# A graph network on one core: list products spread over a chunk, and nine subtractions moved to GpSimd

## The chip, the cores and the metric

The kernel runs on one core of one Trainium2 chip. What is compared is the device time of one execution, in microseconds. Four compute engines matter here: TensorE (PE in the profile), VectorE (DVE), ScalarE (ACT) and GpSimd (POOL); SyncE (SP) only issues transfers. Each engine works through its own queue in order and waits where an instruction needs another engine's or a transfer's result.

## The reference

The graph has 2708 nodes with 512 features each and a symmetric 0/1 matrix `adj` in which about 0.6% of the entries are ones. Four layers follow each other, and each ends with a residual sum and a layer norm. Layers 0, 1 and 3 are plain graph convolutions. The change touches layer 2, which is attention applied twice:

```python
def _gat_layer(x, W, adj):
    proj = x @ W
    Wh, Ws = jnp.split(proj, 2, axis=-1)
    scores = Wh @ Ws.T
    a = jax.nn.softmax(scores, axis=-1) * adj
    out = a @ Wh
    out = out + x
    return jax.nn.leaky_relu(out, NEG_SLOPE)
```

The softmax runs over all 2708 columns before the mask is applied, so all scores are needed; only the product `a @ Wh` can use that the masked matrix is nearly empty.

## The kernel before

**Chunks and stages.** The nodes are cut into 22 row blocks of 128 (the last one has 20 rows), and a score matrix is made in six column chunks of 512, 512, 512, 512, 384 and 276 (`CH`). `Attention.layer` runs once for each of the two attention layers and walks the chunks k = 0 to 5; this text calls the work of one chunk a stage. In stage k three things are interleaved in one written order:

- The **scores** of chunk k. Chunks 0 to 4 use a scheme with seven products in place of eight for a pair of row blocks (`pair_steps`), ten pairs in a stage; each pair yields twice "mid" and twice "end", and other work is put in at these points. Some of the summed weights are not kept in SBUF but streamed back in each stage by `load_sums` (the transfers `s<-sums`).
- The **softening** of chunk k-1 (`soften`), one row block at a time: VectorE subtracts the chunk's column maxima (`shift`) from the scores, ScalarE takes the exponential one or two steps later, VectorE adds the result to the running sum and multiplies it with the mask, and SyncE writes the block to DRAM (`pairs<-s`). There are 26 steps (`SOFT`), the first at about the fourth end of the stage, the last near its end.
- The **list products** of chunk k-2 (`weigh`). For each block of 128 columns, lists of neighbours were worked out earlier. `fetch` gathers, for one list, 128 rows of `pairs` by an indirect transfer from GpSimd's queue (`g<-pairs,givers`), and `weigh` multiplies the gathered weights with the gathered rows into an accumulator (`acc<-g`). A block has four lists that stand alone and two groups of four, so six products and twelve gathers; a chunk of 512 has four blocks, 24 products and 48 gathers. `end` scales the finished block and adds the residual on VectorE.

So the products of a chunk can't begin before the whole chunk was softened and written, which is at the end of the stage before.

**The written order.** The program keeps a clock of its own (`advance`, `self.clock`), which adds an estimate for each TensorE product, 0.85 us for a single list and 1.1 us for a group. `fetch` puts down when a gather should have landed: 1.15 us after the gather before it, plus 6, and for the first gather of a chunk 16 us more. `weigh` puts a product into TensorE's queue only if that estimate has passed, and it is called up to three times at each "end". At most ten gathers stand ahead of their products (`AHEAD = WIDES - 1`, with eleven buffers). A gather's buffer is that of the gather eleven before it, so on the chip it also waits for that one's product. The clock sets only the order of the queues; what runs when is decided by the waits.

**The rest of the layer.** In stage 5 and after it (called the tail here) there is the softening of chunks 4 and 5 and the lists of chunks 3 to 5. Between them the first layer's tail puts the projections of the second layer (`second`), and the second layer's tail the first products of the last graph layer (`early`). The softening of chunk k writes into the DRAM buffer that chunk k-2's gathers read, so it waits for these in the written order (`while self.chunks[ch.k - 2].to_fetch`, and `chunks[-3]` in the tail).

Of the kernel before, what the change touches and what calls it, by code (L numbers as in the profile page):

```python
# [22 lines left out]
NB = 22  # L23
# [458 lines left out]
def pairs_of(k):  # L482


    return {4: (1, P), 5: (1, P)}.get(k, (2, 2 * P))


STREAMED = 4
SOFT = NB + 2 * 2
ALONE = 18  # L490
SEVEN = [k for k in range(len(CH)) if CH[k][1] >= 384]
# [884 lines left out]
class Chunk:  # L1376


    def __init__(self, ly, k):
        self.ly, self.k, self.cw = ly, k, CH[k][1]  # L1380
        self.name = f"{ly.number}_{k}"
        self.blocks = blocks_of(k)
        self.s, self.masks, self.ends = {}, {}, []
        self.half = self.cw // 2
        self.seven = k in SEVEN
        self.part, self.complete, self.ready, self.top = {}, [], [], None
        self.softened = 0
        self.apart = 2 if self.seven else 1
        self.fetched, self.rden = [], None
        self.x, self.first = {}, {}  # L1390
        self.rows = set()
        self.mv = None

        self.to_weigh = []
        for q, (i, _, _) in enumerate(self.blocks):
            ts = lists_of(i)
            self.to_weigh += [(q, t, t is ts[0], t is ts[-1]) for t in ts]
        self.to_fetch = [(q, t) for q, ts, _, _ in self.to_weigh for t in ts]
        self.first_fetch = self.to_fetch[0]
# [9 lines left out]
class Attention:  # L1409
# [7 lines left out]
    def __init__(self, fast):  # L1417
        self.f, self.k, self.nc = fast, fast.k, fast.nc
        self.page, self.bank = fast.page, fast.bank
        tc = self.k.tc  # L1420
        self.scratch = self.k.ctx.enter_context(
            tc.tile_pool(name="pairs", bufs=1, space=DRAM)
        )

        self.pairs = [
            [
                self.scratch.tile([NP, 2 * PAIR + D], FP, tag=f"p{a}{b}", name=f"pairs{a}{b}")
                for b in range(2)  # L1430
            ]
            for a in range(2)
        ]
        self.mixed = self.scratch.tile([DC, P, D], FP, tag="mixed", name="mixed")
        self.quarter = [
            [
                self.scratch.tile(
                    [2, P, pairs_of(k)[0] * P], FP, tag=f"q{a}_{k}", name=f"quarter{a}_{k}"
                )
                for k in range(len(CH))  # L1440
            ]
            for a in range(2)
        ]
        self.sums = [
            [
                self.scratch.tile([3, P, 2, 2 * P], FP, tag=f"u{a}_{k}", name=f"sums{a}_{k}")
                for k in range(STREAMED)
            ]
            for a in range(2)
        ]  # L1450
        self.layers = [AttentionLayer(a, self.pairs[a]) for a in range(2)]
        self.clock, self.fetch_free, self.pending = 0.0, 0.0, []
        self.left = None


    def blank(self):
# [140 lines left out]
    def sum_weights(self, ly, k):  # L1597
# [6 lines left out]
        names = ("s1", "s2", "s4")  # L1604
        if k < STREAMED:
            ly.streamed[k] = [self.page(f"{n}_{a}_{k}", FP, (P, 2, wide)) for n in names]
# [273 lines left out]
    def soften(self, ch):  # L1880


        nc, v, cw = self.nc, ch.softened, ch.cw
        ch.softened += 1
        if v < NB:
            n = rows_of(v)
            s = ch.s[v][:n, :cw]
            nc.vector.tensor_sub(s, s, ch.shift[:n, :cw])
        j = v - ch.apart
        if 0 <= j < NB:  # L1890
            s = ch.s[j][: rows_of(j), :cw]
            nc.scalar.activation(s, s, AF.Exp)
        j -= ch.apart
        if j < 0:
            return
        if j == NB - 1:
            ch.softened = SOFT
        if j == 0 and ch.k >= 2:
            while self.chunks[ch.k - 2].to_fetch:
                self.weigh(True)  # L1900
        if j % DC == 0 and j + 2 * DC < NB:
            self.load_mask(ch, j // DC + 2)
        n = rows_of(j)
        s = ch.s[j][:n, :cw]
        if j == 0:
            ch.sum = self.page(f"sum{ch.name}")
            nc.vector.tensor_copy(ch.sum[:, :cw], s)
        else:
            nc.vector.tensor_add(ch.sum[:n, :cw], ch.sum[:n, :cw], s)
        nc.vector.tensor_mul(s, s, ch.masks.pop(j)[:n, :cw])  # L1910
        to = ch.ly.pairs[ch.k % 2][j * P : j * P + n, :]
        if cw == BANK:
            nc.sync.dma_start(
                to[:, : 2 * PAIR].rearrange("j (r x) -> j r x", x=PAIR)[:, :, D:],
                ch.s[j][:n, :].rearrange("j (r x) -> j r x", x=2 * P),
            )
            return
        for r in range(2):
            w = min(2 * P, cw - r * 2 * P)
            nc.sync.dma_start(  # L1920
                to[:, r * PAIR + D : r * PAIR + D + w],
                ch.s[j][:n, r * 2 * P : r * 2 * P + w],
            )
# [17 lines left out]
    def fetch(self, ch):  # L1941


        q, t = ch.to_fetch.pop(0)
        g = self.f.wide(f"g{ch.name}_{q}_{t}")
        i, _, w = ch.blocks[q]

        for b in (q, q + 1):
            self.load_rows(ch, b)

        h = t // ONLY if t < QUARTERS * ONLY else (QUARTERS - 1, 0)[q % 2]
        first, width = (D + P + h * QW, D + P - h * QW) if q % 2 else (0, D + (h + 1) * QW)
        self.nc.gpsimd.indirect_dma_start(
            out=g[:, :width],
            out_offset=None,
            in_=ch.ly.pairs[ch.k % 2][:, :],
            in_offset=bass.IndirectOffsetOnAxis(ap=self.k.givers[:, i, t : t + 1], axis=0),
            element_offset=(q // 2) * PAIR + first,
        )

        begin = max(self.fetch_free, self.clock + (16 if (q, t) == ch.first_fetch else 0))
        self.fetch_free = begin + 1.15
        ch.fetched.append((g, self.fetch_free + 6))

# [8 lines left out]

    def fetch_ahead(self):
        count = sum(len(c.fetched) for c in self.chunks)
        for c in self.chunks:
            while c.to_fetch:
                if c.softened < SOFT or count >= self.AHEAD:
                    return
                self.fetch(c)  # L1980
                count += 1
# [11 lines left out]
    def weigh(self, wait=False):  # L1993

        nc = self.nc
        self.fetch_ahead()
        ch = next((c for c in self.chunks if c.to_weigh), None)
        if ch is None:
            return False
        q, ts, first, last = ch.to_weigh[0]  # L2000
        if len(ch.fetched) < len(ts):
            return False
        if ch.fetched[len(ts) - 1][1] > self.clock and not wait:
            return False
        ch.to_weigh.pop(0)
        if ch.rden is None:
            self.divisor(ch)
        w = ch.blocks[q][2]
        gs = [ch.fetched.pop(0)[0] for _ in ts]
        if first:  # L2010
            ch.acc = self.bank(1, f"acc{ch.name}_{q}")
            if ch.ly.number == 1:
                ch.first[q] = self.page(f"x1{ch.name}_{q}")
                self.nc.sync.dma_start(ch.first[q][:w], self.k.saved[1][ch.blocks[q][0]][:w])
        for h, g in enumerate(gs):
            lo, m = (0, w) if len(gs) == 1 else (h * QW, QW)
            e, z = (0, P - lo) if q % 2 else (D + lo, 0)
            nc.tensor.matmul(
                ch.acc[lo : lo + m],
                g[:, e : e + m],  # L2020
                g[:, z : z + D],
                start=first,
                stop=last,
            )
        self.advance(cost(D) if len(gs) == 1 else 1.1)
        if last:
            a = (ch, q, ch.acc, ch.x.pop(q), ch.first.pop(q, None))
            self.later(1.5, lambda: self.end(*a))
        self.fetch_ahead()
        return True  # L2030
# [86 lines left out]
    def layer(self, ly, chunks, fill):  # L2117
        f = self.f
        self.chunks, self.made = chunks, {}
        for k, ch in enumerate(chunks):  # L2120
            old = chunks[k - 1] if k else None
            following = chunks[k + 1] if k + 1 < len(chunks) else None

            n = -1
            for what in self.walk(ch):
                if what == "mid":
                    if old and n >= 3 and old.softened < SOFT:
                        self.soften(old)
                    continue
                n += 1  # L2130
                if old and n < 2:
# [19 lines left out]
                        self.restore(ly, i)  # L2151
                self.greatest(ch)

                for _ in range(3):
                    if not self.weigh():
                        break
                if old and n == 2:
                    self.shift_rows(old)
                if old and n == 3:
                    self.shift_columns(old)  # L2160
            assert not old or old.softened == SOFT
        last = chunks[-1]
        self.load_mask(last, 0)
        self.load_mask(last, 1)
# [122 lines left out]
```

## Time and profile before

| | |
|---|---|
| time, median of 3 runs | 2297.17 us (2293.18 to 2298.72) |
| the profiled execution's own time | 2341.13 us |
| its span | 2339.0 us |
| TensorE, share of the span | 96% |
| VectorE, ScalarE, GpSimd | 66%, 31%, 31% |
| granted TensorE clock, mean | 0.985 |
| first attention layer, stages 0 to 5 begin at | 761.5, 829.4, 900.8, 1005.0, 1107.2, 1184.2 us |
| second attention layer, stages 0 to 5 begin at | 1467.6, 1532.2, 1605.8, 1710.8, 1813.3, 1888.9 us |

The stages' beginnings are the first matmuls of each chunk's block 18, which is computed alone, or of block 0 in stage 5. A line of the table by stages, as the prediction shows it, gives a stretch of the execution, its length, then for each engine the time that it was busy and the number of its instructions that began in it, the granted TensorE clock, the mean busy share of the sixteen DMA engines, and the GB/s that they moved. In a line of the timeline the last bracket is the time that the engine stood idle ahead of the instruction, and what ended the wait; "issue" means nothing that the profile shows. As nearly all operations are recorded through one helper, all have its line number (L71), and they are told apart by the tiles that they write and read.

### The profile page before, as it was taken

How to read it: one execution, taken by the hardware profiler on the slowest of the kernel's cores; microseconds unless marked ns; L12 is line 12 of the kernel's file. 1: busy time of each engine (PE TensorE's matmuls, PEld its weight loads, DVE VectorE, ACT ScalarE, POOL GpSimd, SP SyncE). 2: the span in 40 equal slices, each digit the busy share in tenths (PEclk: the TensorE clock that was granted, in tenths of full speed). 3: DMA queues.
4: the chain of work that ended last, by engine and by line, in shares of the span. 5: the costliest groups of instructions: out<-in, count | busy, mean ns of one | idle time of the engine just before them, and what ended most of it. 6: DMA issues, size and time to landing. Idle time of an engine off the chain costs nothing.

```text
span 2339.0 us, 29486 instructions
## 1 busy us (share of the span) xinstructions
PE 2237.2 (96%) x9724; PEld 1515.8 (65%) x9724; DVE 1547.5 (66%) x3180; ACT 725.9 (31%) x1654; POOL 717.8 (31%) x827
## 2 busy tenths in 40 slices
PE   9999999999999998999999999998998997899997
PEld 6776876777545786566764345787565763466685
DVE  6777787777655679778784512579888896354523
ACT  7444452222111243233332101243233332251221
POOL 2433521111000002635566450002634564643000
PEclk9999999999999999999999999999999998999999
DMA  9966752223576426968899998426978899884311
GB/s 346 283 186 189 205 148 76 79 77 115 194 262 253 157 77 205 335 218 318 293 362 360 341 399 333 169 78 210 330 243 286 307 306 343 265 249 148 110 47 42
DMA packets 285139, 523.27 MB, mean 224 GB/s; under 512 B 42926, under 2 KB 134758, under 8 KB 284976
## 3 DMA queue, kind: packets, MB, share of 16 engines
q1 hardware_dynamic: 216320, 306.34, 37.9%
q0 software_dynamic: 68656, 214.96, 27.6%
q8 instruction: 78, 1.28, 0.2%
q14 instruction: 85, 0.70, 0.1%
HBM read 335.34 MB, written 185.83 MB: 223 GB/s over the span
## 4 chain that ended last, share of the span: by engine, by line
PE 71%; DVE 13%; issue 6%; DMA 6%; ACT 2%; POOL 1%; SPq 1%; another core or an unknown queue 0%; DVEq 0%; ACTq 0%; POOLq 0%
PE acc L71 27%; PE spx L71 10%; PE mm L71 8%; PE spy L71 8%; PE z L71 6%; PE wst L71 6%; DVE s L71 5%; PE sp L71 3%; DVE sum L71 2%; DMA at<-in_adj_t 1%; DVE top L71 1%; DMA g<-pairs,givers 1%; DMA x<-in_x 1%; DMA x<-x 1%; DVE r L71 1%
## 5 line engine op out<-in xcount | busy, mean ns | idle before, releaser
L71 POOL DMA_INDIRECT g<-pairs,givers x510 | 535.8, 1051 | 912.5 <-issue 359.3
L71 PE MATMUL acc<-m,xh 128*128 128x512 f32 (+4 forms) x1584 | 566.1, 379 | 8.4 <-issue 7.0
L71 PE MATMUL acc<-m,xl 128*128 128x512 f32 (+4 forms) x1584 | 549.5, 365 | 11.0 <-DVE xl L71 9.4
L71 PEld LDWEIGHTS acc<-m,xh 128*128 128x128 f32 (+1 forms) x1584 | 288.1, 188 | 71.9 <-issue 28.6
L71 PEld LDWEIGHTS acc<-m,xl 128*128 128x128 f32 (+1 forms) x1584 | 288.3, 188 | 54.7 <-DVE xl L71 10.4
L71 PE MATMUL acc<-g 128*32 128x512 f32 (+1 forms) x1020 | 285.0, 610 | 12.2 <-DMA g<-pairs,givers 7.5
L71 PE MATMUL mm<-w,ht 128*128 128x512 f32 (+1 forms) x528 | 223.3, 593 | 0.0
L71 ACT CAST m<-at 128x512 fp32r<-128x512 uint8 (+5 forms) x396 | 199.1, 567 | 40.2 <-DMA at<-mask 20.1
L71 PE MATMUL spx<-xs,wst_sb 128*128 128x256 f32 (+1 forms) x800 | 201.3, 375 | 9.2 <-DVE s L71 9.1
L71 PEld LDWEIGHTS spx<-xs,wst_sb 128*128 128x128 f32 x800 | 149.3, 193 | 47.2 <-issue 14.8
L71 DVE TENSOR_TENSOR s<-s,shift 128x512 f32<-128x512 f32 (+3 forms) x264 | 162.4, 619 | 24.7 <-ACT shift L71 14.4
L71 ACT ACTIVATE s<-s 128x512 f32<-128x512 f32 (+3 forms) x264 | 152.0, 582 | 84.8 <-DVE s L71 74.7
L71 DVE TENSOR_TENSOR s<-s,a 128x512 f32<-128x512 f32 (+3 forms) x264 | 166.0, 629 | 18.5 <-issue 9.5
L71 PEld LDWEIGHTS acc<-g 128*32 128x32 f32 (+1 forms) x1020 | 79.7, 136 | 148.5 <-issue 107.4
L71 PEld LDWEIGHTS mm<-w,ht 128*128 128x128 f32 (+1 forms) x528 | 95.8, 186 | 116.6 <-issue 112.3
L71 ACT COPY s<-spx 128x256 f32<-128x256 f32 (+1 forms) x300 | 106.0, 361 | 196.0 <-PE spx L71 143.5
L71 DVE TENSOR_TENSOR sum<-sum,s 128x512 f32<-128x512 f32 (+4 forms) x252 | 156.3, 620 | 4.1 <-ACT s L71 4.1
L71 DVE TENSOR_TENSOR top<-top,s 128x512 f32<-128x512 f32 (+4 forms) x240 | 149.6, 623 | 13.7 <-ACT s L71 9.6
L71 PE MATMUL z<-w,xt 128*128 128x512 f32 (+1 forms) x352 | 151.4, 596 | 0.0
L71 PE MATMUL wst<-xt,mixed 128*128 128x512 f32 (+2 forms) x384 | 150.9, 545 | 0.0
L71 PE MATMUL spy<-xs,wst_sb 128*128 128x256 f32 (+1 forms) x480 | 121.9, 377 | 9.4 <-DVE s L71 9.2
L71 PE MATMUL sp<-xs,wst_sb 128*128 128x276 f32 (+5 forms) x512 | 129.1, 460 | 0.0
(190 smaller groups left out, 2686.3 us busy)
## 6 DMA issues: line engine op xcount, KB each, us to landing
pairs<-z_sb SPq DMA_DIRECT2D x84, 768.0 KB
pairs<-s SPq DMA_DIRECT2D x168, 256.0 KB
s<-sums SPq DMA_DIRECT2D x96, 256.0 KB
at<-in_adj_t SPq DMA_DIRECT2D x84, 256.0 KB
xres<-x POOLq DMA_DIRECT2D x44, 256.0 KB
x<-o POOLq DMA_DIRECT2D x43, 256.0 KB
pairs<-s SPq DMA_DIRECT2D x84, 128.0 KB
a<-mask SPq DMA_DIRECT2D x40, 256.0 KB
```

Of the source, the lines that this page charges most:

```text
L71: ins = call(*args, **kw)
```

## The change

- Subtractions: of the 22 blocks of chunks 0 to 3 (512 columns, `STREAMED = 4`), the blocks 4, 6, ..., 20 (`OTHERS`, nine of them) are subtracted on GpSimd. The instruction is put into GpSimd's queue four softening steps before VectorE would have done it (`OTHERS_AHEAD`).
- Spacing: in stages 2, 3 and 4 (`SPACING`) a list product may not be written before `next_list`, which advances by 1.5, 1.5 or 1.2 us of the written clock for each list of a product. In these stages products are also written at "mid", one each, and two in place of three at "end".
- Gathers: in these stages at most six stand ahead of their products in the written order, in place of ten (`EVEN_AHEAD`). The number of buffers stays eleven.
- The first gather of a chunk, in all stages, is taken to land 5 us late in place of 16 (`FIRST_LANDS`).

```diff
+OTHERS, OTHERS_AHEAD = range(4, NB - 1, 2), 4
+FIRST_LANDS = 5
+SPACING, EVEN_AHEAD = {2: 1.5, 3: 1.5, 4: 1.2}, 6
...
+        self.others = set(OTHERS) if k < STREAMED else ()
...
-            nc.vector.tensor_sub(s, s, ch.shift[:n, :cw])
+            if v not in ch.others:
+                nc.vector.tensor_sub(s, s, ch.shift[:n, :cw])
+            if v + OTHERS_AHEAD in ch.others:
+                s = ch.s[v + OTHERS_AHEAD][:, :cw]
+                nc.gpsimd.tensor_sub(s, s, ch.shift[:, :cw])
...
-        begin = max(self.fetch_free, self.clock + (16 if (q, t) == ch.first_fetch else 0))
+        begin = max(self.fetch_free, self.clock + (FIRST_LANDS if (q, t) == ch.first_fetch else 0))
...
+        most = EVEN_AHEAD if self.spacing else self.AHEAD
...
-                if c.softened < SOFT or count >= self.AHEAD:
+                if c.softened < SOFT or count >= most:
...
+        if self.spacing and not wait:
+            if self.clock < self.next_list:
+                return False
+            self.next_list = max(self.next_list, self.clock - 2) + self.spacing * len(ts)
...
+            self.spacing = SPACING.get(k, 0.0)
             for what in self.walk(ch):
                 if what == "mid":
                     if old and n >= 3 and old.softened < SOFT:
                         self.soften(old)
+                    self.weigh()
                     continue
...
-                for _ in range(3):
+                for _ in range(2 if self.spacing else 3):
                     if not self.weigh():
                         break
```

More of the change, by code (lines that the diff above doesn't have):

```diff
@@ L1453, in __init__ @@
         self.left = None
+        self.spacing, self.next_list = 0.0, 0.0
     def blank(self):
@@ L2161, in layer @@
             assert not old or old.softened == SOFT
+        self.spacing = 0.0
         last = chunks[-1]
```

## The prediction

> **What bounds the kernel now.** The page first: TensorE is busy for 96% of the span, so the question is where its time isn't products. The stage table comes next (stages 1 to 5 of the first attention layer, then two pieces of its tail).
>
> ```profile
> PE 2237.2 (96%) x9724; PEld 1515.8 (65%) x9724; DVE 1547.5 (66%) x3180; ACT 725.9 (31%) x1654; POOL 717.8 (31%) x827
> ...
> 829.40:900.80 71.40, 66.71 (x305) 55.04 (x304) 61.87 (x104) 31.77 (x75) 0.00 (x0) 1.00 0.35 107
> 900.80:1005.00 104.20, 96.20 (x409) 65.47 (x408) 83.62 (x142) 30.59 (x74) 51.23 (x48) 0.95 0.79 279
> 1005.00:1107.20 102.20, 97.11 (x425) 66.40 (x424) 78.79 (x134) 32.64 (x78) 49.54 (x48) 0.98 0.82 288
> 1107.20:1184.20 77.00, 72.73 (x394) 58.34 (x394) 63.79 (x115) 29.62 (x78) 40.92 (x38) 0.96 0.85 304
> 1184.20:1245.00 60.80, 59.70 (x272) 40.18 (x271) 51.34 (x108) 20.40 (x50) 37.38 (x35) 1.00 0.98 357
> 1245.00:1320.00 75.00, 69.17 (x213) 29.76 (x211) 39.04 (x94) 15.88 (x36) 39.35 (x39) 0.95 0.96 342
> 1320.00:1467.60 147.60, 147.60 (x446) 65.39 (x445) 31.51 (x61) 13.59 (x28) 46.44 (x49) 1.00 0.95 359
> ```
>
> A stage has a floor. Stage 0 of the second layer, with nothing but scores, takes 64.6 us and is 64.56 busy. Three single lists take 2.68 us in the chain (0.87 each; a group and two singles 2.91, so the group about 1.2): 24 products are 16 x 0.87 + 8 x 1.2 = 23.5. With 3 us of transposes, stages 2 and 3 need 91 us and take 104.2 and 102.2; in the second layer 105.0 and 102.5. Stage 1 needs 65 and takes 71.4 and 73.6. Some 60 us are lost in all, and stage 4 adds to it.
>
> How they are lost: cutting stage 1 and the start of stage 2 into tens shows VectorE full, and a later ten shows it idle beside full DMA engines.
>
> ```profile
> 860.00:870.00 10.00, 10.00 (x48) 8.81 (x47) 9.82 (x17) 5.58 (x14) 0.00 (x0) 1.00 0.65 196
> 901.00:911.00 10.00, 6.17 (x21) 3.60 (x20) 9.76 (x18) 1.71 (x4) 0.00 (x0) 1.00 0.39 125
> ...
> 971.00:981.00 10.00, 6.58 (x26) 3.23 (x24) 2.58 (x4) 0.90 (x2) 6.72 (x7) 0.97 0.92 307
> 981.00:991.00 10.00, 9.25 (x25) 6.29 (x26) 9.22 (x15) 3.41 (x9) 5.18 (x5) 0.69 0.99 364
> ```
>
> TensorE's timeline names the waits, GpSimd's its rhythm:
>
> ```profile
> 910.82 1.13 PE L71 MATMUL spx<-xs,wst_sb 128*128 128x256 f32 x4 [3.83 <-DVE s L71]
> 981.75 2.08 PE L71 MATMUL spy<-xs,s 128*128 128x256 f32 x4 [3.77 <-issue]
> 1024.75 1.65 PE L71 MATMUL spy<-xs,s 128*128 128x256 f32 x3 [3.38 <-issue]
> 1809.87 1.65 PE L71 MATMUL spx<-t,wst_sb 128*128 128x256 f32 x3 [4.66 <-ACT v L71]
> ...
> 1142.52 0.95 POOL L71 DMA_INDIRECT g<-pairs,givers  x1 [17.87 <-PE acc L71]
> 1975.59 0.95 POOL L71 DMA_INDIRECT g<-pairs,givers  x1 [18.99 <-PE acc L71]
> ```
>
> So there are two kinds. VectorE is late (first and fourth line; ScalarE's queue holds exponentials that wait for VectorE's subtractions). And the streamed sums (tile s in `spy<-xs,s`, the third product) come late in stretches where gathers come in a burst: the ten from 971 moves 307 GB/s, and at 1024 eleven gathers had just been issued back to back. That it is these transfers is my reading; the view says only "issue". GpSimd's 17.87 us is the other face: eleven gathers at once, then none until the first product.
>
> **What the Trainium skill says.** "SBUF — State Buffer", section Who interferes with whom: a VectorE instruction with two SBUF inputs contends with a GpSimd instruction that reads SBUF; the second to start blocks for the whole of the first. No trace row shows this pair: where GpSimd multiplied before (`xt<-xt,dg`), VectorE ran `ht<-acc,xt`, which has one input in PSUM, and both kept their times. "GPSIMD Engine Reference", section 3.1, gives about 2.6 cycles an element for such an operation; the trace agrees (first line below: 512 columns in 1289 ns, and 276 in 776, hence 2.2 ns a column). "TensorE: Matmul & The Clock Gate", section What's actually happening: after an idle window of about 3.4 us the clock halves. The trace agrees: 3.77 us of waiting, then 0.69 in the next ten. "Trainium Kernel Development and Optimization", section Key Constraints: transfers of all queues share the sixteen DMA engines; the table's 0.92 to 0.99 with sums late fits.
>
> ```profile
> L71 POOL TENSOR_TENSOR xt<-xt,dg 128x512 f32<-128x512 f32 x16 | 20.2, 1289 | 27.0 <-DVE cnt_sb L71 27.0
> L71 DVE TENSOR_TENSOR s<-s,shift 128x512 f32<-128x512 f32 x168 | 114.0, 682 | 23.5 <-ACT shift L71 14.4 <-issue 9.1
> ```
>
> **The change, part by part.**
>
> *Subtractions.* VectorE loses 9 x 0.60 = 5.4 us a stage (0.60 is what one takes from start to start in the timeline; 0.68 is its latency), in eight stages. GpSimd gains 9 x (1.25 + 0.1). Without contention that is 5.4 us off a full VectorE. With the exclusive port, 82% of VectorE's busy time in stage 1 is in two-SBUF-input operations (50.7 of 61.5: subtractions, sums, mask products, maxima, `s<-s,v`), so a GpSimd subtraction costs VectorE 0.82 x 1.25 = 1.03 us and saves 0.60: a loss of 3.8 a stage. On the path this counts in stage 1 of both layers, where VectorE is full from 850 to 911. Bounds for both: -11 and +8. I take -2: the page states the block outright, but a GpSimd instruction also starts inside VectorE's short gaps and one-input operations. GpSimd's queue: a subtraction stands behind gathers that wait only for products five or more back, so it isn't held; four steps are some 8 us of lead. Gathers behind it come 1.35 us later, hidden by those already landed.
>
> *Spacing.* Reckoned by the written clock, the products of stages 2 and 3 lay from 24 to 78 of 86 us and now begin at 11. With six ahead, a second group of four finds two of its gathers outstanding; the other two land 2 x 1.15 + 6 = 8.3 us later by the estimate, so group follows group by 10 us, not 6, and a block takes 24. Three blocks fit in stage 2, not four: 6 products are carried out of it, 10 out of stage 3, 18 out of stage 4 (7 before) and 19 out of stage 5 (13 before). Gathers per stage drop from 48 to about 38 in stage 2, and the fill of eleven at a stage's start shrinks, as old gathers hold buffers. That should cure most late sums in the first layer: 3.8 + 3.1 of clock at 981; 3.4 + 1.7 at 1024; 3.7 + 3.1 in stage 4 (clock 0.96 of 77 us); 2 for lists: 21. In the second layer some 8 of the same kind. I take two thirds, -19. Of the 8.0 us lost to "ACT v" waits there, plus 3.4 of clock, a third: -4.
>
> *Earlier first product.* In stage 2 the first gather left at 911.4, 10.6 us into the stage, held by the last `pairs<-s`, and one landing lasts 5.6 us in the chain. A product written at 11 us then stands in front of the scores until about 16. Cost 0 to 10 for the two layers: +4.
>
> *Carried products.* TensorE's work only moves. But six products more go into the tail with twelve gathers. In the first layer the tail's projections hide them (TensorE 147.6 of 147.6); DMA at 0.95 leaves little, +1. In the second the gathers run at 1.26 us each from 1975 to 2036 and TensorE waits for them: 12 x 1.26 = 15, less the 6.4 that the products took in earlier stages, and less what the 19 us gap at 1975.6 can take in: 0 to +15, +4.
>
> Sum: -2 - 19 - 4 + 4 + 5 = -16 on the profiled 2341.1, 0.7%. That execution is 1.9% above the median; on the runs it is 2297 - 16 = **2281 us**, its own range 2268 to 2291.
>
> **The rivals.**
>
> *No contention.* The rows where both engines worked speak for it, though they are of another pair. Then -11 and not -2, and VectorE's lateness in the second layer goes too (-11, not -4): 2265.
>
> *Full contention eats the gain.* The page and the 82% speak for it. +8 and not -2, and none of the -4: 2297 - 2 = 2295, the same.
>
> *The spread stays on paper.* Only buffers hold GpSimd back on the chip, and there are still eleven; gathers could burst as before. Against it: carried lists fill the buffers at stage starts. Then only a third of the 19: 2294, the same.
>
> *Slower: the tails pay.* DMA is at 0.95 to 0.98 from 1184 to 1467. Stage 5 begins with 36 gathers outstanding in place of 16. If the second layer pays all of 12 x 1.26 = 15, and the first 20 more gathers at 0.9 us of DMA time each = 18 (128 rows of some 600 floats, 0.31 MB; queue 0 spends 27.6% of 2339 us on 215 MB), the tails cost 33 and not 5: 2281 + 28 = 2309. It decides once the tails cost more than the 21 that the stages win.
>
> **How the numbers follow.** A measurement of this kernel can't tell less than 0.3%, 7 us, from no change. Chances: likeliest 0.45 (0.40 faster, 0.05 same), no contention 0.18 (faster), full contention 0.12 (0.09 same, 0.02 faster, 0.01 slower), on paper 0.08 (0.05 same, 0.02 faster, 0.01 slower), tails 0.17 (slower). Faster 0.62, same 0.19, slower 0.19. The range runs from 2251 (no contention, all of the 29 for late sums, first products that cost nothing) to 2312 (the tails' 2309 and the 3 us by which the runs scatter), and leaves out about a tenth on either side.
>
> **What would show it.** VectorE's two-input operations keep 0.68 us beside GpSimd's subtractions, or grow towards 1.9. Stage 1 gets shorter than 71.4 and 73.6, or doesn't. The 3 to 5 us waits at `spy<-xs,s` are gone and the DMA share of stages 2 to 4 is even over tens. Stages 2 and 3 take some 90 us, of which 6.4 is only carried. From stage 5 on each layer is longer. I am wrong if the stages' gain comes back as waits for `g` in the tails, or if stage 1 grows.

## The result and the profile after

The changed kernel takes 2368.5 us (2366.9 to 2370.0, 4 runs) where the kernel before takes 2295.2 (2288.2 to 2298.7, 4 runs): the ratio is 1.0323, with an interval from 1.0296 to 1.0351. It is 73 us slower. The forecast was 2281 us, 16 faster.

The profiled execution of before that the prediction read took 2341 us, 44 more than its runs. So the kernel before was profiled anew (e3 below); that execution took 2296.7 us, with a span of 2294.6, and is what the changed kernel (span 2365.7) is compared with here.

The page of the changed kernel, its first part:

```profile
PE 2244.0 (95%) x9724; PEld 1515.2 (64%) x9724; DVE 1583.6 (67%) x3108; ACT 730.8 (31%) x1654; POOL 815.7 (34%) x899
```

VectorE has 72 instructions fewer than before and is busy for longer: 1583.6 us against 1547.5.

The table by stages of the changed kernel, with the columns of the prediction's table (stretch, length, busy time and instructions of TensorE, its weight loads, VectorE, ScalarE and GpSimd, granted clock, DMA share, GB/s). The lines are stages 1 to 4 of the first layer, all from its stage 5 to the second layer, and the second layer's stage 4 and all from its stage 5 to the end:

```profile
828.30:903.50 75.20, 68.72 (x305) 56.18 (x304) 67.56 (x101) 32.57 (x75) 14.98 (x9) 0.98 0.36 109
903.50:996.80 93.30, 88.49 (x386) 63.27 (x385) 83.58 (x123) 31.74 (x75) 57.19 (x52) 0.96 0.84 281
996.80:1085.20 88.40, 88.11 (x409) 63.93 (x406) 80.80 (x121) 33.30 (x78) 56.83 (x50) 1.00 0.87 294
1085.20:1167.70 82.50, 74.56 (x398) 57.33 (x397) 70.95 (x111) 29.72 (x77) 48.65 (x42) 0.96 0.84 283
1167.70:1476.50 308.80, 292.72 (x963) 139.67 (x961) 123.63 (x265) 49.97 (x113) 140.05 (x140) 0.97 0.95 344
...
1802.80:1891.50 88.70, 75.61 (x381) 57.14 (x380) 81.58 (x132) 30.02 (x76) 48.88 (x42) 0.92 0.82 266
1891.50:2365.70 474.20, 426.99 (x1741) 270.81 (x1739) 219.81 (x486) 120.73 (x261) 155.51 (x168) 0.96 0.55 186
```

The same of the kernel before, profiled anew (stages 2 to 4, the first layer's tail, stage 4 of the second layer, and the rest):

```profile
911.20:1004.90 93.70, 91.89 (x409) 63.30 (x408) 81.46 (x137) 31.03 (x74) 52.08 (x48) 1.00 0.86 304
1004.90:1100.00 95.10, 94.26 (x426) 65.20 (x425) 78.17 (x132) 33.04 (x78) 50.65 (x48) 1.00 0.86 307
1100.00:1170.20 70.20, 69.38 (x393) 55.77 (x392) 64.21 (x115) 30.11 (x78) 43.56 (x40) 1.00 0.96 338
1170.20:1444.00 273.80, 273.15 (x924) 133.88 (x922) 121.85 (x262) 49.65 (x113) 122.17 (x121) 1.00 0.98 366
...
1777.20:1851.40 74.20, 68.87 (x377) 53.95 (x377) 69.07 (x129) 29.17 (x75) 45.70 (x40) 1.00 0.93 331
1851.40:2294.60 443.20, 408.62 (x1701) 266.48 (x1699) 216.21 (x479) 120.76 (x261) 133.88 (x148) 0.97 0.55 185
```

Read the two side by side, and three things stand out.

| | before (e3), us | after, us | difference |
|---|---|---|---|
| first layer, stage 1 | 74.0 | 75.2 | +1.2 |
| first layer, stages 2 to 4 | 93.7 + 95.1 + 70.2 | 93.3 + 88.4 + 82.5 | +5.2 |
| first layer, from stage 5 | 273.8 | 308.8 | **+35.0** |
| second layer, stage 1 | 72.7 | 75.3 | +2.6 |
| second layer, stages 2 to 4 | 100.3 + 95.6 + 74.2 | 91.9 + 94.5 + 88.7 | +5.0 |
| second layer, from stage 5 to the end | 443.2 | 474.2 | **+31.0** |

These are 80 us; the stretch ahead of the attention layers, whose code is the same, was 9 shorter (it lies between 759 and 771 us over all profiles here), which gives the 71 between the spans. First, stages 2 and 3 of the first layer take 93.7 and 95.1 us before, near the floor of 91, with the clock at 1.00: the 104.2 and 102.2 of the prediction's table are not what the runs beside the change do. Second, products were taken out of stages 2 to 4, and together these don't get shorter: stages 2 and 3 lose 7.1 us in the first layer and 9.5 in the second, and stage 4 gains 12.3 and 14.5. In the first layer 1193 matmuls remain of 1228, but TensorE's busy time falls by only 4.4 us (251.2 of 255.5), with clocks of 0.96 in stages 2 and 4. Third, the tails get all that was carried, 39 matmuls and 19.6 us busy in the first, and more.

What TensorE waited for in the changed kernel (waits view: engine, tile, what ended the wait; us in total, times, the longest):

```profile
PE acc L71 <- DMA g<-pairs,givers: 29.8, 33, 12.3
PE spy L71 <- DVE s L71: 29.3, 14, 4.5
PE acc L71 <- ACT m L71: 17.8, 6, 15.9
```

The same rows of the kernel before in e3:

```profile
PE acc L71 <- ACT m L71: 12.3, 5, 6.0
PE spy L71 <- DVE s L71: 8.9, 4, 3.5
PE acc L71 <- DMA g<-pairs,givers: 7.0, 18, 0.7
```

And the timeline of the changed kernel at the two longest waits, one in each tail (five lines of four engines, out of one execution):

```profile
1357.16 0.95 POOL L71 DMA_INDIRECT g<-pairs,givers  x1 [18.62 <-DMA y<-r]
1364.33 6.11 PE L71 MATMUL acc<-g 128*128 128x512 f32 x7 [12.28 <-DMA g<-pairs,givers]
...
1973.37 0.56 DVE L71 TENSOR_TENSOR s<-s,a 128x384 f32<-128x384 f32 x1 [16.04 <-DMA a<-mask]
1974.40 0.20 ACT L71 ACTIVATE rs_t<-rs_v 128x4 f32<-128x4 f32 x1 [22.22 <-DVE rs_v L71]
1979.45 0.79 PE L71 MATMUL acc<-m,xh 128*128 128x512 f32 x1 [15.85 <-ACT m L71]
```

The first pair is the first product of chunk 5. Its gather left at 1357.2, 2.5 us after SyncE had issued the last writes of the softened chunk, and landed seven microseconds later; the product had been put in front of the projections that could have filled these 12 us. The other three are a chain: VectorE waits 16 us for a mask that comes late among the gathers (the DMA engines are 95% busy here), ScalarE's layer norm `rs_t` waits behind that, the cast `m` stands behind the layer norm, and TensorE waits for `m`.

### The profile page after: what moved, and what is told of

Same layout as the page of the kernel before. It is cut to its first block, busy times and chain, and to the rows that moved or that the text cites. A ratio compares the mean times of both kernels' runs of the same rounds, so it can differ in the third digit from the quotient of the medians.

```text
span 2365.7 us, 29512 instructions
## 1 busy us (share of the span) xinstructions
PE 2244.0 (95%) x9724; PEld 1515.2 (64%) x9724; DVE 1583.6 (67%) x3108; ACT 730.8 (31%) x1654; POOL 815.7 (34%) x899
## 4 chain that ended last, share of the span: by engine, by line
PE 62%; DVE 19%; DMA 12%; issue 4%; ACT 1%; POOL 1%; SPq 0%; DVEq 0%; POOLq 0%; ACTq 0%
PE acc L71 25%; PE mm L71 8%; PE spx L71 8%; DVE s L71 8%; PE spy L71 6%; PE wst L71 6%; PE z L71 5%; DVE sum L71 4%; DMA g<-pairs,givers 4%; DMA pairs<-s 3%; PE sp L71 2%; DVE top L71 2%; DMA a<-mask 2%; DMA x<-x 1%; DMA x<-in_x 1%
## 5 line engine op out<-in xcount | busy, mean ns | idle before, releaser
L71 PE MATMUL acc<-m,xh 128*128 128x512 f32 (+4 forms) x1584 | 565.5, 378 | 18.7 <-ACT m L71 17.8
L71 PE MATMUL acc<-g 128*32 128x512 f32 (+1 forms) x1020 | 297.6, 613 | 30.5 <-DMA g<-pairs,givers 29.8
L71 POOL TENSOR_TENSOR s<-s,shift 128x512 f32<-128x512 f32 x72 | 101.8, 1438 | 367.7 <-ACT shift L71 367.3
L71 DVE TENSOR_TENSOR sum<-sum,s 128x512 f32<-128x512 f32 (+4 forms) x252 | 168.3, 668 | 2.7 <-ACT s L71 2.6
L71 DVE TENSOR_TENSOR top<-top,s 128x512 f32<-128x512 f32 (+4 forms) x240 | 153.6, 640 | 11.9 <-ACT s L71 7.6
L71 DVE TENSOR_TENSOR s<-s,shift 128x512 f32<-128x512 f32 (+3 forms) x192 | 138.8, 728 | 17.4 <-ACT shift L71 17.4
```

The lines of the kernel that those rows point to most:

```text
L71: ins = call(*args, **kw)
```

## The experiments

Diffs are against the changed kernel where they begin with its constants, otherwise against the kernel before. The versions were timed in five series, each with the kernel before beside them, and ratios are to it in the same series. In the series of e10 to e15 and in that of e20 and e21 the kernel before itself took 2345 and 2349 us, in the other three 2288 to 2293, so times are compared only within a series, or between two whose kernels before agree.

**e3: the kernel before, profiled again.** No edit.

> The kernel before, once more, for a second profiled execution. The first had 2341 us against 2295 in its runs. If profiling slows this kernel where transfers are dense, the span is again near 2340, with waits in other places of stages 2 to 4 of either layer; if that execution was an odd one, it is near 2297 and stages 2 and 3 take some 92 to 98 us, not 102 to 105. Then what the lists' order could win there was never in the runs.

2294.5 us, ratio 1.0008 (0.9995 to 1.0020). Its stages are in the table above. Three of TensorE's waits in the first profile:

```profile
PE spy L71 <- issue: 13.0, 7, 3.8
PE acc L71 <- issue: 12.5, 17, 7.0
PE acc L71 <- DMA g<-pairs,givers: 7.5, 11, 2.4
```

Of the waits at "issue" nothing is left in e3, and of the 8.7 us at "ACT v" 4.4. So most of what the prediction meant to cure isn't in the kernel as it was timed beside the change. It was no stray execution either. TensorE waits at "issue" for 16 to 29 us in seven traces, the first profile and all six of the two series at 2345 and 2349 (e10, e11, e12, e15, e20, e21), and not at all in the thirteen others. The same seven hold some 30% fewer semaphore records (27,251 in the first profile, 38,636 in e3), and their view of DMA issues gives no transfer's landing. So the first profile most likely shows the condition of these two series. And "issue" in it can stand for a transfer whose landing was not recorded; that it was the sums is not shown.

**e1: the subtractions alone.**

```diff
-FIRST_LANDS = 5
-SPACING, EVEN_AHEAD = {2: 1.5, 3: 1.5, 4: 1.2}, 6
+FIRST_LANDS = 16
+SPACING, EVEN_AHEAD = {}, 6
...
-                    self.weigh()
                     continue
```

> Only the nine subtractions of chunks 0 to 3 go to GpSimd; lists are written as before (16 us, ten ahead, no spacing). Port theory (the exclusive port makes each GpSimd subtraction cost VectorE about 1.2 us where it saves 0.6, so some 4 to 5 us in each of eight stages where VectorE is nearly full, and gathers queue behind it): 25 to 45 us slower, 2320 to 2340. Tail theory (the carried lists are what costs): within 10 us of before, at most stage 1 longer by 4 us in each layer. In the profile: two-input VectorE operations beside a GpSimd subtraction take 1.4 us or more, stage 1 is 75 us in both layers.

2335.5 us, ratio 1.0184 (1.0158 to 1.0210): 45 us slower, with every list where it was. Stages 2 to 4 grow by 21.9 us in the first layer and 16.3 in the second, stage 1 by 1.1 and 2.5, the tails by 0.9 and 0.8. One row from VectorE's groups (count, busy us, mean ns) and one from TensorE's waits:

```profile
L71 DVE TENSOR_TENSOR s<-s,shift 128x512 f32<-128x512 f32 x96 | 74.0, 777 | 6.6 <-ACT shift L71 6.6
...
PE acc L71 <- DMA g<-pairs,givers: 23.2, 28, 2.7
```

Both doubts of the prediction show. VectorE's busy time in stages 1 to 4 of both layers goes from 596 to 630 us although 72 subtractions of 0.60 have left it: 34 + 43 = 77 us are lost, 1.07 for each subtraction on GpSimd. And the waits for gathers rise from 7.0 to 23.2 us.

**e7: VectorE keeps all 22.** GpSimd multiplies the nine blocks by ones in place, so that it reads SBUF at the same places, and takes nothing from VectorE. The values stay as they are.

```diff
             nc.vector.tensor_sub(s, s, ch.shift[:n, :cw])
+            if ch.k < STREAMED and v + 4 in range(4, NB - 1, 2):
+                s = ch.s[v + 4][:, :cw]
+                nc.gpsimd.tensor_mul(s, s, self.k.ones.to_broadcast([P, ch.cw]))
```

> The kernel before, with VectorE keeping all 22 subtractions, and GpSimd multiplying the same nine blocks by ones in place, four steps ahead (two inputs read from SBUF, values unchanged). This is the cost of the shared port by itself. Port theory: VectorE pays about 1.2 us for each, 9 x 1.2 = 11 us a stage in eight stages, where it has 5 to 10 us of slack in some: 45 to 85 us slower than before, that is the 45 of the subtractions alone and some of the 5.4 us a stage that these saved. If it isn't the port but GpSimd's queue (gathers behind subtractions) that cost 45, this is again 40 to 50 slower and VectorE's operations keep 0.68 us.

2334.3 us, ratio 1.0188 (1.0161 to 1.0214): as slow as e1. VectorE has all its subtractions here, and GpSimd's operations are shorter (1.10 us on average, in e1 1.40). So the 43 us of subtractions taken off VectorE bought little, and most of the 45 is the price of the work on GpSimd; as the two kinds of operation differ in length and run at different moments, the exact split isn't shown. In stage 1 the multiplications ran ahead of VectorE's full stretch, and stage 1 kept its length (73.9 and 72.6), yet the total is the same: stages 2 to 4 of the two layers are 43.5 us longer than in e3. So the place where the prediction looked for the cost, stage 1, holds little of it.

**e10 and e20: only GpSimd's queue.** VectorE keeps all 22; at each of the nine places GpSimd writes a small constant twelve times, reading nothing.

```diff
+        self.idle = tile_("idle", [P, 16], FP)
...
+            if ch.k < STREAMED and v + 4 in range(4, NB - 1, 2):
+                for _ in range(12):
+                    nc.gpsimd.memset(self.k.idle, 0.0)
```

> The kernel before, with GpSimd kept busy for about 1.2 us at the places of its nine subtractions by twelve small writes of zeros that read nothing from SBUF (VectorE keeps all 22 subtractions). If the shared read port is what the subtractions cost, this is within 15 us of before and VectorE's operations keep 0.68 us. If GpSimd's queue is what costs (gathers behind the subtractions), it is 30 to 45 slower, as with the subtractions alone, and products wait as often for g.

> The kernel before, VectorE keeps all 22 subtractions, and at each of the nine places GpSimd writes twelve small constants, some 1.2 us that read no SBUF. Only the gathers queued behind are later, by as much as behind a subtraction. If the cost of the subtractions is the shared port alone, this is within 0.3% of the kernel before; if it is the gathers' queue alone, it costs as much as the subtractions in e21; if both, it lies between, at 0.4% to 1.4%.

**e21: the subtractions alone again**, in the series of e20.

> The nine subtractions on GpSimd and nothing else, beside the kernel that only writes, on one chip. As before, 1.8% slower than the kernel before.

e10 has 1.0121 (1.0084 to 1.0159), e20 1.0189 (1.0130 to 1.0247), and e21 1.0067 (1.0025 to 1.0109). Of e20, the row of VectorE's groups, two of the waits, and stages 2 to 4 of the first layer:

```profile
L71 DVE TENSOR_TENSOR s<-s,shift 128x512 f32<-128x512 f32 x168 | 114.0, 682 | 12.0 <-ACT shift L71 8.4 <-issue 3.6
...
PE acc L71 <- DMA g<-pairs,givers: 36.4, 32, 3.1
PE acc L71 <- issue: 8.1, 7, 5.6
...
907.00:1017.90 110.90, 101.20 (x410) 65.59 (x409) 83.85 (x142) 30.77 (x74) 63.47 (x156) 0.95 0.78 262
1017.90:1133.40 115.50, 107.29 (x425) 68.47 (x424) 80.19 (x136) 32.57 (x78) 62.17 (x156) 0.96 0.77 256
1133.40:1222.70 89.30, 78.14 (x394) 60.08 (x393) 67.87 (x122) 29.88 (x78) 54.74 (x149) 0.92 0.85 293
```

VectorE's subtractions keep their 682 ns, so the port is out of it, and still the kernel is slower. The trace to hold beside this one is the first profile, with the same waits at "issue", and not e3: these stages are 32.3 us longer than there, those of the second layer 21.2, and the waits for `g` are 36.4 us where the first profile has 7.5. The twelve writes follow each other at 0.168 us, 2.0 us in all, and so hold the gathers half as long again as a subtraction (1.40 us in e1); they are the larger dose. What this shows is that GpSimd work between gathers costs by the queue alone, with waits for `g` of 35 to 36 us. How the subtractions' own cost divides between queue and port isn't shown: the doses differ, and e21 cost 0.7% where e1, in a series with a faster kernel before, cost 1.8%.

**e8 and e17: the spacing alone,** ten ahead, first gathers at 16, nothing on GpSimd.

```diff
-OTHERS, OTHERS_AHEAD = range(4, NB - 1, 2), 4
-FIRST_LANDS = 5
-SPACING, EVEN_AHEAD = {2: 1.5, 3: 1.5, 4: 1.2}, 6
+OTHERS, OTHERS_AHEAD = (), 4
+FIRST_LANDS = 16
+SPACING, EVEN_AHEAD = {2: 1.5, 3: 1.5, 4: 1.2}, 10
```

> Spacing and products at mid alone: ten ahead, first gather 16 us late as before, all subtractions on VectorE. By its written order 10 gathers of chunk 2 are left for stage 5 (16 before, 36 in the changed kernel). If even products help, 2275 to 2288; if evenness is worth nothing, 2288 to 2296; if the carried gathers at stage starts (4 in stages 3 and 4) or products at mid cost, 2300 or more.

> The spacing alone (16 us, ten ahead, no subtraction on GpSimd) beside the three others of this call. As before 0.8% faster than the kernel before; on a chip where the kernel before takes 2340 us and more, 1% to 2%.

2270.2 us, ratio 0.9924 (0.9899 to 0.9949), and 2272.9, 0.9906 (0.9878 to 0.9934). This version is faster than both kernels. Stages 2 and 3 of the second layer and all from its stage 5, in e17:

```profile
1572.50:1663.40 90.90, 89.33 (x402) 62.78 (x401) 84.61 (x144) 31.43 (x75) 50.18 (x48) 1.00 0.88 311
1663.40:1753.90 90.50, 90.44 (x413) 63.16 (x410) 84.24 (x151) 33.29 (x76) 50.18 (x48) 1.00 0.93 319
...
1833.20:2265.80 432.60, 402.00 (x1688) 265.49 (x1686) 213.90 (x475) 120.79 (x260) 131.98 (x142) 0.97 0.55 185
```

Stages 2 and 3 stand at the floor of 91, where e3 has 100.3 and 95.6, and all from stage 5 on is 10.6 shorter. By the written order 10 gathers are carried into stage 5 in place of 16, and GpSimd has 142 instructions there in place of 148. The second layer's stage 4 is 5.1 us longer, and the first layer is as long as in e3.

**e6: first gathers at 5 us, alone.**

```diff
-        begin = max(self.fetch_free, self.clock + (16 if (q, t) == ch.first_fetch else 0))
+        begin = max(self.fetch_free, self.clock + (5 if (q, t) == ch.first_fetch else 0))
```

> The kernel before with one number changed: the first gather of a chunk is taken to land 5 us late, not 16. Four gathers of chunk 2 are left for stage 5 in place of 16. If a product written at 11 us waits in front of the scores, each of stages 2 to 4 shows 2 to 5 us of waiting for g and the time is 2295 to 2315; if the gathers are there in time, and because less is left for the tails, 2275 to 2290.

2306.7 us, ratio 1.0070 (1.0044 to 1.0096): 18 us slower. The first layer's tail is 14.6 longer than in e3, with a wait of 9.5 us for a gather, as in the changed kernel; stages 2 to 4 are 8.4 and 14.0 longer, and the second layer's tail is 17.8 shorter.

**e5 and e18: spacing and 5 us, ten ahead.** e8 with `FIRST_LANDS = 5`.

> The lists' new order with ten gathers ahead and all subtractions on VectorE: nothing carried into stage 5 by its written order (36 gathers with six ahead, 16 before). If the limit of six is what costs in the list part (2341 with it), this is 2285 to 2305. If the early and even products themselves cost, it stays at 2325 to 2340. If the parts simply add, it is the ten-ahead run with subtractions (2342) less the 45 that the subtractions alone cost: 2297.

> The spacing with 5 us for all chunks, ten ahead, no subtraction on GpSimd, as the other end for the kernel with 5 us in the tails alone: 35 to 40 us slower than the spacing alone if the cost of the first lands is the same on every chip; less than 15 us if it was a matter of that chip.

2309.9 us, 1.0094 (1.0070 to 1.0119), and 2316.5, 1.0094 (1.0067 to 1.0121). Beside e8 and e17 in the same series, the 5 us cost 40 and 44 us. Where, two more kernels tell.

**e16: 5 us only for chunks 3 to 5,** whose lists run from stage 5 on; otherwise e5.

```diff
-(FIRST_LANDS if (q, t) == ch.first_fetch else 0)
+((FIRST_LANDS if ch.k >= 3 else 16) if (q, t) == ch.first_fetch else 0)
```

> Even spacing, ten gathers ahead, no subtraction on GpSimd; the first gather of a chunk is counted as landing at 5 us for chunks 3 to 5 alone, whose lists run from stage 5 on, and at 16 us for chunks 0 to 2. If the 40 us that the 5 us added to the even spacing are a cost of the tails, where a product is written in front of work that could have covered its gather, this kernel is 25 to 40 us slower than the spacing alone and close to the kernel with 5 us for all chunks. If they are a cost of the stages 2 to 4, it is within 8 us of the spacing alone.

2289.4 us, 0.9978 (0.9957 to 1.0000): 16.5 slower than e17. The first tail is 10.4 us longer than there and the second 3.8. The other 27 of the 44 come, by difference, with chunks 0 to 2, in stages 2 to 4. One of the waits in e16's first tail (the longest, in the second, is 6.2 us):

```profile
1317.97 5.31 PE L71 MATMUL acc<-g 128*128 128x512 f32 x8 [2.71 <-DMA g<-pairs,givers]
```

For the stages, e18's profile gives the mechanism in the second layer. At the end of stage 2 TensorE waits for ScalarE's eviction `s<-spx`, and that stands behind a layer norm that waits for VectorE (two engines' timelines of e18):

```profile
1696.74 0.21 ACT L71 ACTIVATE rs_t<-rs_v 128x4 f32<-128x4 f32 x1 [7.50 <-DVE rs_v L71]
...
1697.26 2.08 PE L71 MATMUL spx<-xs,wst_sb 128*128 128x256 f32 x4 [7.20 <-ACT s L71]
```

The end of stage 3 has the same (6.38 us). With the lists early, the last product of the stage begins 15 us ahead of its end in place of 0.5 in e17, so the block's layer norm falls among the last scores and nothing is left to fill the wait. The two stages are 11.9 and 8.0 us longer than in e17.

**e11: 5 us only for chunks 0 to 2,** the counterpart of e16, in another series.

```diff
-(FIRST_LANDS if (q, t) == ch.first_fetch else 0)
+((FIRST_LANDS if ch.k < 3 else 16) if (q, t) == ch.first_fetch else 0)
```

> Spacing with ten ahead and all subtractions on VectorE, and the first gather 5 us late for chunks 0 to 2 alone (whose lists begin in stages 2 to 4), 16 us for chunks 3 to 5 (whose lists begin in the tail). With 5 everywhere it was 2310, with 16 everywhere 2270. If the early product costs in the tails (the 12 us wait for g in the first layer's), this is 2275 to 2290; if it costs in the stages, 2300 to 2310.

2317.7 us beside a kernel before of 2345.1: 0.9878 (0.9817 to 0.9939). In this series, where the traces look like the one that the prediction read, the even lists win more than the early products cost in the stages. There is no spacing alone beside it, so it doesn't size that cost.

**e2: all three changes of the lists** (spacing, 5 us, six ahead), nothing on GpSimd: `OTHERS = ()`.

> Only the lists' order is changed (5 us, spacing, six ahead); all subtractions stay on VectorE. Port theory: as fast as before or faster, 2280 to 2300. Tail theory: the 36 gathers carried into stage 5 in place of 16 are all still there, so 40 to 60 us slower, 2335 to 2355, with the waits for gathers and rows at the end of each layer. If both count, each of the two runs has a part and the parts sum to about 73.

2340.8 us, 1.0215 (1.0183 to 1.0248). Against e5 six ahead adds 1.2%, some 28 us. All from stage 5 of the second layer on, in e5 and then in e2:

```profile
1872.20:2305.90 433.70, 395.21 (x1669) 265.12 (x1667) 213.06 (x473) 120.98 (x261) 133.51 (x139) 0.97 0.52 180
```

```profile
1862.90:2336.90 474.00, 426.47 (x1741) 270.63 (x1739) 219.87 (x486) 120.56 (x261) 155.34 (x168) 0.97 0.55 186
```

The stages 2 to 4 ahead of it are 20.5 us shorter in e2 (260.0 against 280.5), the rest is 40.3 longer. By the timeline GpSimd issues 139 gathers from stage 5 on in e2 and 111 in e5. Where they follow each other without a wait, most take 1.26 us (0.95 and a pause of 0.30), so as an estimate 28 x 1.26 = 35 us. In the changed kernel and e3 it is 139 and 119, by the same estimate 20 x 1.26 = 25 of the 31 us. In the first layer e2's stages 2 to 4 win 10.4 and its tail loses 25.7.

**e4: the changed kernel with ten ahead.** `EVEN_AHEAD = 10`.

> The changed kernel with ten gathers ahead in place of six in the spaced stages. By its written order nothing of chunk 2 is left for stage 5 (36 gathers in the changed kernel, 16 before). Tail theory: the tails get short again, 2290 to 2310. Port theory: still 2335 to 2365. In the profile: stage 5 to the end of each layer is 20 us or more shorter than in the changed kernel, stages 2 to 4 are longer by the products that they take back (some 10 us).

2341.9 us, 1.0222 (1.0194 to 1.0250): with the subtractions too, going back to ten wins 1.0% of the 3.2. The tails take 284.6 and 435.7 us in place of 308.8 and 474.2, while stages 2 to 4 take back 17.3 and 16.4.

**e12: six ahead in stages 2 and 3, ten in stage 4,** nothing on GpSimd. By the written order 16 gathers are carried into stage 5, as before the change, in place of 36.

```diff
-        most = EVEN_AHEAD if self.spacing else self.AHEAD
+        most = EVEN_AHEAD if self.spacing > 1.3 else self.AHEAD
```

> The lists' new order with six ahead in stages 2 and 3 and ten in stage 4, all subtractions on VectorE: 16 gathers of chunk 2 are left for stage 5 (none with ten everywhere at 2310, 36 with six everywhere at 2341). If the products carried into the tails are what the six cost, this is a half or less of the way: 2310 to 2326. If six ahead costs in stages 2 and 3 themselves, it stays at 2330 to 2345.

2313.1 us, 0.9863 (0.9821 to 0.9906), no slower than e11, though it also has the 5 us for chunks 3 to 5. So six ahead in stages 2 and 3 costs nothing that shows here. With e2's table, where the stages win and the tail loses, this points to the carry into stage 5 as the cost; a version with ten throughout and 5 us everywhere was not timed in this series.

**e15 and e19: the subtractions with the spacing,** ten ahead and 16 us.

```diff
-FIRST_LANDS = 5
-SPACING, EVEN_AHEAD = {2: 1.5, 3: 1.5, 4: 1.2}, 6
+FIRST_LANDS = 16
+SPACING, EVEN_AHEAD = {2: 1.5, 3: 1.5, 4: 1.2}, 10
```

> The changed kernel with two numbers set back: first gather 16 us late, ten ahead; the subtractions on GpSimd and the spacing stay. Without the subtractions it was 2270. If these cost the same 45 whatever stands around them, 2310 to 2318; if an evener stage hides a part of the port's cost, 2285 to 2305; below 2270 if they help once the gathers are even.

> The spacing with the nine subtractions on GpSimd, 16 us, ten ahead. If a subtraction costs VectorE and the gathers' queue what it cost on the old lists, it is 30 to 45 us slower than the spacing alone. If even lists leave GpSimd free time between gathers and cure the half of the cost that came from gathers queued behind subtractions, it is 10 to 25 us slower.

e15 has 0.9953 (0.9924 to 0.9981), e19, in the series of e17, 2302.4 us, 1.0038 (1.0024 to 1.0051). In e19's series the spacing alone is 29.5 us faster: the subtractions cost less than the 45 of e1, but they cost more than the spacing wins. In e19 the waits for `g` are 8.1 us against 5.3 in e17, those of scores for VectorE 31.5 against 17.6. With even lists the queue hardly shows, and VectorE's lateness does.

## Why the prediction was wrong

By ratios to the kernel before, the parts one on top of the other are: spacing -0.8% (e8), first gathers at 5 us +1.7 (e5), six ahead +1.2 (e2), subtractions +1.1 (the changed kernel): +3.2%. Against the prediction's sum:

| step | predicted, us | measured, us |
|---|---|---|
| Subtractions | -2 (-11 to +8) | +45 alone, +29.5 with the spacing, +1.1% on top of all |
| Spacing | -19 and -4 | -18 and -20, by another way |
| Earlier first product | +4 (0 to 10) | +18 alone, +40 and +44 with the spacing |
| Carried products | +1 and +4 | six ahead, +1.0% (e4) to +1.2% (e2), 23 to 28 us |

**Subtractions.** "SBUF — State Buffer", section Who interferes with whom, was right, and so was the size drawn from it: 1.03 us of VectorE for each subtraction, 1.07 measured in e1. What failed is "On the path this counts in stage 1 of both layers". The six other stages lengthen most, 38 of e1's 45 us, though VectorE is idle for part of them. And "Gathers behind it come 1.35 us later, hidden by those already landed" was false on the old lists: e1 waits 16 us more for `g`. VectorE's sums in the first profile, then two of its groups and a moment of stage 2 in the changed kernel, show the block:

```profile
L71 DVE TENSOR_TENSOR sum<-sum,s 128x512 f32<-128x512 f32 x160 | 109.5, 684 | 0.0
...
L71 DVE TENSOR_TENSOR sum<-sum,s 128x512 f32<-128x512 f32 x160 | 121.5, 759 | 0.0
L71 DVE TENSOR_TENSOR s<-s,shift 128x512 f32<-128x512 f32 x96 | 90.2, 946 | 17.4 <-ACT shift L71 17.4
...
953.27 4.87 DVE L71 TENSOR_TENSOR sum<-sum,s 128x512 f32<-128x512 f32 x1
953.86 3.72 POOL L71 TENSOR_TENSOR s<-s,shift 128x512 f32<-128x512 f32 x3
```

The means were 684 and 682 before. One sum of 0.68 us took 4.87, and ended half a microsecond behind the last of three subtractions. The bound of +8 was no bound, since it covered two stages of eight and left out the queue.

**Spacing.** That the total is near the forecast is luck. The step summed waits of one execution (3.8 + 3.1 and so on) that e3 doesn't have. What the spacing wins in the runs is the second layer's stages 2 and 3, 14.5 us of which stage 4 gives 5.1 back, and 10.6 from stage 5 on, where fewer gathers arrive. Only the small term holds as it was reasoned: the 4.4 us at "ACT v" that e3 has are gone in e17. The step also took the spacing and six ahead for one thing; apart, one wins and the other loses more. The sign of a warning was in the text, "That execution is 1.9% above the median", and the prediction subtracted a gain read from it from the median all the same.

**Earlier first product.** The mechanism, a product written in front of work that could cover its gather, was right and was looked for in stage 2 alone. e16 finds 16.5 us of it in the tails, where chunk 5's product waits 12.28 us in the changed kernel. The 27 in the stages exceed the term because the early lists leave the stage's end bare, which the prediction didn't see.

**Carried products.** The rival "the tails pay" had the count that the step should have used: 36 gathers into stage 5 in place of 16, at 1.26 us each. The step itself counted at stage 5's end, 12 gathers, and let them hide. The tails are 66 us longer than in e3 in place of 5; some 12 of these are the early first product's wait. The rival gave 2309 and still missed: it priced the tails at 33 us where they cost 66, and kept a gain of 21 us in the stages, where stages 2 to 4 of the table cost 10.

Of the signs listed, those against came true: VectorE's operations grew, stage 1 grew to 75.2 and 75.3, the tails got waits for `g`. "TensorE: Matmul & The Clock Gate", section What's actually happening, holds here as well: where the waits are longest the clock falls, 0.78 between 1950 and 1980 us around the 15.85 us wait.

What stays open: how the subtractions' cost divides between port and queue, and why the kernel before takes 2.4% longer in some series (two series on one chip gave 2293 and 2349). The changed kernel as a whole was not timed in such a series; there e11 and e12, with most of its new order of the lists and no subtraction moved, are 1.2 and 1.4% faster than the kernel before.

## What to carry to other kernels

Check that the profiled execution takes what the runs take before its waits are summed into a gain; if it doesn't, they may belong to another condition than the runs. Work that is moved out of a stage is paid at the price of the place where it arrives, here 1.26 us a gather in tails with no cover, and the count to use is what crosses the border, not what is left at the end. An instruction given to an idle engine can delay whatever stands behind it in that queue, and if the two engines share a port, it can take its own length from the other engine; here it did so in every stage, and not only where that engine was full.

## What the runs showed of the hardware

A VectorE operation blocked by GpSimd didn't get in between three subtractions that followed each other: it took 4.87 us across all three. In stage 1 the two engines' instructions alternated, each of VectorE's took some 1.75 us, as in the first two lines here, and GpSimd's nine took 1.66 each, where the three above took 1.24:

```profile
844.42 1.75 DVE L71 TENSOR_TENSOR s<-s,shift 128x512 f32<-128x512 f32 x1
846.09 1.75 DVE L71 TENSOR_TENSOR top<-s,s 128x512 f32<-128x512 f32 x1
842.45 14.98 POOL L71 TENSOR_TENSOR s<-s,shift 128x512 f32<-128x512 f32 x9 [176.23 <-ACT shift L71]
```

Twelve GpSimd writes of 16 columns, 0.11 us each, took 2.0 us in the queue, and 72 groups of them slowed the kernel by 1.2 to 1.9%, with VectorE's subtractions at the 682 ns that they take without them.
